# A GNN layer on one Trainium2 core: raw groups 112 chunks apart, in-degrees counted from 656 bytes at a looked-up place, fewer chunks by columns and rows

## The chip, the cores and the metric

The kernel runs on one core of one Trainium2 chip. TensorE (PE) multiplies matrices, VectorE (DVE) and ScalarE (ACT) work element by element, GpSimd (POOL) issues the indirect DMAs that gather rows by index, and SyncE (SP) issues plain DMAs. Each engine takes its instructions in program order and waits for others through semaphores. The metric is the device time of one execution, in microseconds (us); lower is better.

## The reference

`x` holds 12500 rows of 128 values, `src` and `dst` 200000 edges sorted by `dst`. With H = 512:

```python
h = max(layernorm(x), 0)
agg = segment_sum(h[src], dst, 12500)
deg = segment_sum(ones, dst, 12500)
agg = agg / max(deg, 1)
a = relu(agg @ Wg + h @ Ws + bg)
a = tanh(a @ W1 + b1)
a = tanh(a @ W2 + b2)
out = x + a @ W3 + b3
```

## The kernel before

**Set-up.** `windowed` normalises `x` into a table `htab` in DRAM (lines 205 to 290) and turns the edge indices into columns of 128. The edges are cut into 1563 chunks of 128. As `dst` is sorted and has 16 edges for a node on the average, chunk c falls into a narrow window of nodes around 8c (`window`, 144 nodes wide at first). `htab` is ready some 95 us after the start.

**One chunk.** Its 128 source rows are brought to SBUF, VectorE builds a one-hot matrix of the destinations in the window (`onehot`, L438, eight chunks at a time, three buffers), and TensorE multiplies rows by one-hot and adds the product to the block's sums in PSUM (`add`; all matmuls show as L342 and all transposes as L345, the lines of a helper). A block is 512 nodes; the last ones are smaller.

**Four ways to bring rows.**

- Gathered: POOL issues one indirect DMA for the chunk (`gather`, L352, tile `rows`), at most `AHEAD` = 19 chunks ahead. The pool `rows_in` has that many buffers, and a buffer is free when the chunk's `add` is done.
- Raw: ten groups of eight chunks, `STEP` apart from chunk 256 on, are gathered from `x` itself (L167) before `htab` is there, and normalised on VectorE during chunks 16 to 95 (`centre`, L209 to L216).
- By rows: SP issues 128 plain DMAs of one row each (`row_loads`, tile `srows`; all plain DMAs after the set-up show as L348). It reads the addresses 32 at a time into registers (`offsets`, L363, TENSOR_LOAD). Four buffers.
- By columns: ScalarE or VectorE copies 128 columns out of `tab`, a transposed table in SBUF, with addresses from registers (`column_copies`, L398), and TensorE transposes the result (`turn`).

`LANES` says which of every eighth chunk goes to which of the last two ways: S rows, A ScalarE, V VectorE, - gathered. `load_times` spreads the loads of a lane over the chunks before their use: it takes the places of the lane's chunks in the order of the gathered ones, extends them to the front by `SBUFS - 1` steps for the row lane, and clamps each due time to at least 1. In chunk c all that is due by the count `behind` of gathered chunks done is issued.

**The table `tab`.** `own(s)` (SP) loads 512 rows of `htab` into a tile `xb`, two buffers; `own_turned(s)` transposes it on TensorE, ScalarE copies it to `tab`. Before, this is done for one block in every fourth chunk, from chunk 2 on.

**In-degrees.** The low byte of each `dst` lies in DRAM (`bytes_at`). For each tile of 128 nodes `seen` (SP) loads, for every node, the 2416 bytes in which its edges must lie, and `tallied` (VectorE, L452) counts the bytes equal to the node's; this comes at every 14th chunk, two tiles ahead. `count` turns degrees into a row for a block. `checked` and `outside` see whether any edge lies outside of its window (then `general`, another routine, runs; it doesn't here).

**MLP and the order of work.** A block's four layers are a generator, `layers`, with planned costs. Up to chunk `QUICK` = 1312 one step of it is emitted in every second chunk (`go_on`). From there on a planner compares `now`, the planned time of TensorE, with `there`, the time at which a chunk's rows are planned to arrive (7.5 + 1.251 for each gather), and emits MLP steps until the rows are there. TensorE's, ScalarE's and SP's instructions in this part keep the order of emission.

Of the kernel before, what the change touches and what calls it, by code (L numbers as in the profile page):

```python
# [22 lines left out]
F32 = mybir.dt.float32  # L23
BF16 = mybir.dt.bfloat16
I32 = mybir.dt.int32
U8 = mybir.dt.uint8
AF = mybir.ActivationFunctionType
ALU = mybir.AluOpType
# [8 lines left out]
GRP = 8  # L37
NRAW = 10
RAW0 = 256
STEP = 40  # L40
AHEAD = 19
LATE = 12
LEAD = 16
QUICK = 1312
EVERY = 8
AT = 3
LANES = "AVASA-AVAVA-SAV"
FROM, UNTIL = 152, 1540
SBUFS = 4
MARGIN = 18  # L50
TOGETHER = 4
# [10 lines left out]

TILE_EVERY = 14
PAST = 255


NCOPY = 4
# [4 lines left out]
def windowed(ctx, tc, x, src, dst, Wg, Ws, bg, W1, b1, W2, b2, W3, b3, out, flag):  # L72
# [26 lines left out]
    def first(w, span=per):  # L99
        return (span - w) // 2  # L100
# [5 lines left out]
        return per * c + first(w), w  # L106

    each = E // N
    low_w, wide_w = first(WINDOWS[0][1]), WINDOWS[0][1]
    back = each * (low_w + wide_w - 1)  # L110
    reads = -(-(back - each * low_w + P) // each) * each
    assert each * N == E and each * per == P and reads <= each * (PAST + 1)
    assert all(first(w) >= low_w and first(w) + w <= low_w + wide_w for _, w in WINDOWS)
    pad_dst = 2 * N // (PAST + 1) * (PAST + 1) + PAST
    assert pad_dst >= 2 * N - PAST and NT * P - N <= P
    ended = (E - (reads - back)) // each
    assert not any(n % (PAST + 1) == PAST and (each * n < back or n > ended) for n in range(N))

    lanes = ([], [], [])
    for i, c in enumerate(c for c in range(AT, NCH, EVERY) if FROM <= c < UNTIL and not raw(c)):  # L120
# [64 lines left out]
    def flat(t):  # L185
        return t.rearrange("p a b -> p (a b)")

    htab = dram.tile([NP, D], F32, name="htab")
    bytes_at = dram.tile([back + NROW * ROW + reads], U8, name="bytes_at")
    tab = const.tile([P, NP], F32, name="tab")  # L190
    scol = const.tile([P, NCOL], I32, name="scol")
    ROWB = 4 * D
# [3 lines left out]
    oh_bufs = [const.tile([P, GRP, WINDOWS[0][1]], F32, name=f"oh{i}") for i in range(OHS)]  # L196
    near = const.tile([P, NRAW, GRP], F32, name="near")
    degs = const.tile([P, NT], F32, name="degs")
    parity = const.tile([P, 2], F32, name="parity")
    for i in range(2):  # L200
        nc.vector.tensor_scalar(parity[:, i : i + 1], jp[:, :1], -1.0, float(i * P), op0=ALU.mult, op1=ALU.add)
# [23 lines left out]
    with tc.tile_pool(name="setup", bufs=1) as sp, tc.tile_pool(name="ln", bufs=2) as ln:  # L225

        def indices(name, a, pad, keep):
            r = sp.tile([NROW, ROW], I32, name="idx_raw")

            nc.vector.memset(r, pad)  # L230
            even = FULL // 16 * 16
            for s0, s1 in ((0, even), (even, FULL)):
                if s1 > s0:
                    nc.scalar.dma_start(r[s0:s1, :], a[s0 * ROW : s1 * ROW].rearrange("(p e) -> p e", e=ROW))
            nc.scalar.dma_start(r[FULL : FULL + 1, :REST], a[FULL * ROW : E].rearrange("(p e) -> p e", p=1))
            if name == "src":
                some = r.rearrange("r (q p) -> r q p", p=P)[:, AT::EVERY]
                for to, step, first_at in zip(places, (ROWB, 4), (0, TAB_AT)):
                    nc.vector.tensor_scalar(to, some, float(step), float(first_at), op0=ALU.mult, op1=ALU.add)
            else:  # L240
                r8 = flat(oh_bufs[0]).bitcast(U8)[:NROW, :ROW]
                nc.scalar.copy(r8, r.bitcast(U8).rearrange("r (e b) -> r e b", b=4)[:, :, 0])
                end = back + NROW * ROW
                nc.scalar.dma_start(bytes_at[back:end].rearrange("(r e) -> r e", e=ROW), r8)
                past = flat(oh_bufs[1]).bitcast(U8)[:1, : max(back, reads)]
                nc.vector.memset(past, PAST)
                nc.scalar.dma_start(bytes_at[:back].rearrange("(o e) -> o e", o=1), past[:, :back])
                nc.scalar.dma_start(bytes_at[end:].rearrange("(o e) -> o e", o=1), past[:, :reads])
            rf = sp.tile([NROW, ROW], F32, name="idx_f")
            nc.vector.tensor_copy(rf, r)  # L250
            for q0 in range(0, CPR, 4):
                p = ps_m.tile([P, 4, P], F32, name="pm")
                for q in range(4):
                    nc.tensor.transpose(p[:, q, :NROW], rf[:, (q0 + q) * P : (q0 + q + 1) * P], ident[:NROW, :NROW])  # L254
                keep(q0, p[:, :, :NROW].rearrange("p q r -> p r q"))
# [91 lines left out]
    def sp_dma(*a):  # L347
        tc.keep_in_program_order(nc.sync.dma_start(*a))  # L348
# [84 lines left out]
    def onehot(g):  # L433
# [7 lines left out]
        )]  # L441
        ohs[g] = oh

    def seen(t):

        w = ed.tile([P, reads], U8, name="nearby", bufs=2)
        sp_dma(w, bass.AP(tensor=bytes_at.tensor, offset=bytes_at.offset + t * P * each, ap=[[each, P], [1, reads]]))
        nearby[t] = w

    def tallied(t):  # L450
        w = nearby.pop(t)
        done = nc.vector.tensor_scalar(  # L452
            w, w, parity[:, t % 2 : t % 2 + 1], None, op0=ALU.is_equal, op1=ALU.add, accum_out=degs[:, t : t + 1]
        )
        if newest:
            tc.add_manual_dep(
                done.ins, newest[0].ins.name,
                mybir.DependencyInfo(mybir.DependencyClass.NoSync, mybir.DependencyReason.DATA), reason="issue_after",
            )
        if t % 4 == 3 or t == NT - 1:  # L460
            d = degs[:, t // 4 * 4 : t + 1]
            nc.vector.tensor_scalar(d, d, 1.0, None, op0=ALU.max)
            nc.vector.reciprocal(d, d)

    def checked():

        u = dloc[:, RAW0:RAW1].rearrange("p (u k) -> p u k", k=STEP)
        wide = WINDOWS[0][1]
        ends = [c for c, _ in WINDOWS[1:]] + [NCH - 1]
        parts = [(dloc[:, :RAW0], wide), (u[:, :, GRP:], wide), (u[:, :, :GRP], W_RAW), (near, wide)]  # L470
        parts += [(dloc[:, RAW1 : ends[0]], wide)]
        parts += [(dloc[:, c0:c1], w) for (c0, w), c1 in zip(WINDOWS[1:], ends[1:])]
        parts += [(dloc[:LAST, NCH - 1 : NCH], WINDOWS[-1][1])]
        k = len(parts)
        ext = const.tile([P, 2, k], F32, name="ext")
        nc.vector.memset(ext, 0.0)
        for i, (part, w) in enumerate(parts):
            rows = LAST if i == k - 1 else P
            axis = AX.XY if len(part.shape) == 3 else AX.X
            nc.vector.tensor_reduce(ext[:rows, 0, i : i + 1], part, axis, ALU.min)  # L480
            nc.vector.tensor_reduce(ext[:rows, 1, i : i + 1], part, axis, ALU.max)
            e = ext[:rows, 1, i : i + 1]
            nc.vector.tensor_scalar(e, e, -1.0, float(w - 1), op0=ALU.mult, op1=ALU.add)
        worst = const.tile([P, 1], F32, name="worst")
        nc.vector.tensor_reduce(worst, ext, AX.XY, ALU.min)
        nc.vector.tensor_scalar(worst, worst, 0.0, None, op0=ALU.is_lt)
        return worst

    def outside(worst):
        p = flat(ps_m.tile([P, 4, P], F32, name="pm"))  # L490
        pe.matmul(p[:1, :1], worst, ident_ones, start=True, stop=True)
        nc.vector.tensor_copy(flag, p[:1, :1])

    reach = [[] for _ in blocks]
    for c in range(NCH):
# [243 lines left out]
    def soonest():  # L739
        two = work[: 2 if len(work) > 1 and work[1][3] < work[0][3] and work[0][4] else 1]  # L740
        return min(two, key=lambda w: max(w[2], now), default=None)
# [12 lines left out]
    own(1)  # L754
    own_turned(0)
    own(2)
    seen(0)
    seen(1)
    onehot(0)
    onehot(1)  # L760
    counted = 0
    for c in range(NCH):
        g = c // GRP
# [2 lines left out]
        if c % GRP == 0 and g + 2 < ngrp:  # L766
            onehot(g + 2)
            if raw((g + 2) * GRP):
                raw_scaled(((g + 2) * GRP - RAW0) // STEP)
            copies, times = loading[2]  # L770
            while times and times[0] <= behind:
                times.pop(0)
                next(copies, 0)
            if g == 2 + NRAW + 2:
                worst = checked()
            if g == 2 + NRAW + 4:
                outside(worst)
            if 2 <= g < 2 + NRAW:
                centre(ed, raw_rows[g - 2], GRP, raw_stats(g - 2), bufs=1)
            if g == 2 + NRAW:  # L780
                factors(stats_raw)
# [15 lines left out]
        if c >= QUICK:  # L797

            there = 7.5 + 1.251 * (NRAW * GRP + order.index(c)) if c not in apart else 0
            while soonest() and max(now, soonest()[2]) < there:  # L800
                go_on(soonest())
            now = max(now, there) + 0.27
# [10 lines left out]

        if c % TILE_EVERY == 1 and c // TILE_EVERY < NT:
            tallied(c // TILE_EVERY)
            if c // TILE_EVERY + 2 < NT:
                seen(c // TILE_EVERY + 2)
        if c % 4 == 2 and c // 4 + 1 < nown:
            own_turned(c // 4 + 1)
            if c // 4 + 3 < nown:  # L820
                own(c // 4 + 3)
        if c < QUICK:
            if c % 2 == 0:
                go_on(work[0] if work else None)
# [380 lines left out]
```

## Time and profile before

| what | before |
|---|---|
| median of 3 runs | 1818.41 us (1816.91 to 1819.31) |
| the profiled execution | 1817.22 us |
| its span, first to last instruction | 1815.4 us |
| mean granted TensorE clock | 0.889 |
| HBM traffic | 147.49 MB read, 13.03 MB written |
| DMA packets | 135577, 163.06 MB |

All times in the profile are those of one execution on the chip. A group's row gives the line in the kernel, the engine, the operation, the tile written and read, the count, the busy time in us and the mean of one in ns, and then how long the engine was idle before these instructions and what ended that. A row of the timeline gives the start and the duration in us; PE rows count two instructions for one matmul in fp32. A row of busy time by stretches gives PE, PEld (weight loads), DVE, ACT and POOL, each with the count of instructions, and then the granted clock, the share of the DMA engines and GB/s. The page's chain of work that ended last gives DMA 26%, PE 24%, issue 20%, ACT 16% and POOL 8%.

### The profile page before, as it was taken

The page shows a single profiled execution, that of the slowest core. Times are in us where ns is not written, and L with a number is a line of the kernel's source. Part 1 is how long each engine was busy: PE and PEld are TensorE (multiplying, and loading weights), DVE is VectorE, ACT ScalarE, POOL GpSimd, SP SyncE. Part 2 cuts the span into 40 slices and gives each one's busy share as a digit, 9 for nine tenths or more (in the row PEclk, how much of TensorE's full clock was granted, in tenths as well). Part 3 has the DMA queues.
Part 4 walks back from the last instruction along what each step waited for, and adds up shares of the span by engine and source line. Part 5 has one row for each costly group of instructions (what it writes and reads, how often), then busy time and mean ns, then how long its engine had stood idle before and what let it go on. Part 6 is the DMA issues. An engine that isn't in the chain of part 4 may idle for free.

```text
span 1815.4 us, 36659 instructions
## 1 busy us (share of the span) xinstructions
PE 1299.8 (72%) x5031; PEld 812.2 (45%) x5031; DVE 1152.6 (63%) x6351; ACT 1187.4 (65%) x10333; POOL 1348.7 (74%) x1429
## 2 busy tenths in 40 slices
PE   0046767777888787877777777777777767698598
PEld 0035544444555554444444444444444344454457
DVE  7946845668677788766756666756666764644411
ACT  1201145867878788878777777778768865777763
POOL 7777777777777777777777777777777776777773
PEclk9996565989898899989999889989889998798899
DMA  8844423233333332332332332332333323222221
GB/s 211 235 140 112 122 68 80 75 81 81 81 94 94 86 102 75 94 88 74 84 84 75 87 88 75 86 82 76 86 81 81 92 71 86 67 72 66 65 59 37
DMA packets 135577, 163.06 MB, mean 90 GB/s; under 512 B 32934, under 2 KB 99107, under 8 KB 135128
## 3 DMA queue, kind: packets, MB, share of 16 engines
q0 software_dynamic: 45472, 93.22, 20.4%
q1 hardware_dynamic: 86574, 63.90, 12.4%
q10 hardware_dynamic: 3276, 3.51, 0.7%
q14 instruction: 213, 1.74, 0.3%
q8 instruction: 42, 0.69, 0.2%
HBM read 147.49 MB, written 13.03 MB: 88 GB/s over the span
## 4 chain that ended last, share of the span: by engine, by line
DMA 26%; PE 24%; issue 20%; ACT 16%; POOL 8%; DVE 3%; ACTq 1%; DVEq 0%; POOLq 0%
DMA rows<-htab,scol 26%; ACT cols L398 14%; PE pm L342 14%; PE agg L342 7%; POOL rows L352 4%; POOL raw L167 4%; PE edge L342 2%; ACT h L416 2%; DVE cols L398 1%; DVE nearby L452 1%; DVE oh L438 1%; ACTq L363 1%; PE pt L345 1%; PE pm L345 0%; DVEq L363 0%
## 5 line engine op out<-in xcount | busy, mean ns | idle before, releaser
L352 POOL DMA_INDIRECT rows<-htab,scol x1341 | 1270.7, 948 | 416.7 <-issue 230.2
L398 ACT COPY cols<-tab 128x4 uint8 x9856 | 996.4, 190 | 283.3 <-issue 231.7
L342 PE MATMUL pm<-h,w 128*128 128x512 f32 (+4 forms) x1344 | 648.3, 580 | 36.1 <-ACT h L416 22.2
L342 PE MATMUL agg<-oh,rows 128*128 128x144 f32 (+3 forms) x1914 | 474.9, 352 | 231.7 <-DMA rows<-htab,scol 224.3
L342 PEld LDWEIGHTS agg<-oh,rows 128*128 128x128 f32 x1914 | 353.6, 224 | 509.1 <-DMA rows<-htab,scol 370.2
L398 DVE COPY cols<-tab 128x4 uint8 x5504 | 432.2, 196 | 164.1 <-issue 142.9
L438 DVE TENSOR_TENSOR oh<-shared,dloc 128x1152 f32<-128x1152 f32 (+2 forms) x186 | 245.7, 1322 | 358.0 <-PE agg L342 217.1
L452 DVE TENSOR_SCALAR_CACHE_REDUCE nearby<-nearby,parity 128x2416 uint8<-128x2416 uint8 x98 | 266.2, 2717 | 4.8 <-DMA nearby<-bytes_at 4.8
L342 PEld LDWEIGHTS pm<-h,w 128*128 128x128 f32 x1344 | 222.1, 204 | 60.2 <-ACT h L416 26.5
L342 PE MATMUL edge<-oh,rows 128*128 128x144 f32 (+2 forms) x768 | 178.6, 332 | 80.9 <-DMA rows<-htab,scol 80.1
L342 PEld LDWEIGHTS edge<-oh,rows 128*128 128x128 f32 x768 | 131.7, 209 | 192.7 <-DMA rows<-htab,scol 126.7
L416 ACT ACTIVATE h<-pm,b2c 128x512 f32<-128x512 f32 (+4 forms) x112 | 70.2, 626 | 63.9 <-PE pm L342 63.8
L419 ACT COPY tab<-pt 128x512 f32<-128x512 f32 (+1 forms) x25 | 14.4, 577 | 127.2 <-PE pt L345 127.2
L167 POOL DMA_INDIRECT raw<-in_x_dram,rsrc x80 | 77.1, 964 | 25.6 <-issue 23.5
L416 ACT ACTIVATE h<-pm,b1c 128x512 f32<-128x512 f32 (+4 forms) x112 | 68.9, 627 | 29.1 <-PE pm L342 28.7
L254 PE MATMUL pm<-ident,idx_f 98*128 98x98 f32 x32 | 6.2, 376 | 77.8 <-DVE agg L220 47.5
L345 PE MATMUL pm<-ident,cols 128*128 128x128 f32 x120 | 35.6, 297 | 32.1 <-DVE rd L511 15.7
L342 PEld LDWEIGHTS agg<-oh,turned 128*128 128x128 f32 x176 | 36.6, 227 | 36.5 <-issue 24.7
L342 PE MATMUL agg<-oh,turned 128*128 128x144 f32 (+1 forms) x176 | 42.4, 328 | 11.3 <-ACT turned L419 11.3
L573 DVE TENSOR_TENSOR mT<-agg,sums 128x136 f32<-128x136 f32 (+6 forms) x57 | 15.2, 271 | 40.6 <-PE agg L342 31.3
L254 PEld LDWEIGHTS pm<-ident,idx_f 98*128 98x128 f32 x32 | 5.1, 223 | 78.6 <-issue 47.8
L688 DVE TENSOR_TENSOR o<-pt,xb 128x512 f32<-128x512 f32 x23 | 15.7, 681 | 35.3 <-PE pt L345 34.9
(90 smaller groups left out, 632.6 us busy)
## 6 DMA issues: line engine op xcount, KB each, us to landing
srows<-htab SPq DMA_DIRECT2D x2816, 0.5 KB
nearby<-bytes_at SPq DMA_DIRECT2D x98, 302.0 KB
rows<-htab,scol POOLq DMA_INDIRECT x1341
xb<-htab SPq DMA_DIRECT2D x24, 256.0 KB
xb<-in_x_dram SPq DMA_DIRECT2D x23, 256.0 KB
out_dram<-o SPq DMA_DIRECT2D x23, 256.0 KB
xt<-in_x_dram SPq DMA_DIRECT2D x7, 704.0 KB
htab<-h SPq DMA_DIRECT2D x7, 704.0 KB
```

Of the source, the lines that this page charges most:

```text
L167: nc.gpsimd.indirect_dma_start(out=t[:, j, :], out_offset=None, in_=x, in_offset=bass.IndirectOffsetOnAxis(ap=rsrc[:, g, j : j + 1], axis=0),)
L342: tc.keep_in_program_order(nc.tensor.matmul(*a, **k))
L345: tc.keep_in_program_order(nc.tensor.transpose(*a, **k))
L352: nc.gpsimd.indirect_dma_start(out=r, out_offset=None, in_=htab, in_offset=bass.IndirectOffsetOnAxis(ap=scol[:, c : c + 1], axis=0),)
L363: loads, vs = nc.values_load_multi_w_load_instructions(places[min(lane, 1)][r : r + 1, q // EVERY, p0 : p0 + LOADS], engines=[kind], min_v ...
L398: done = tc.keep_in_program_order(copy(tb[:, 4 * p : 4 * p + 4], tbytes[:, bass.ds(v - TAB_AT, 4)]))
L416: tc.keep_in_program_order(nc.scalar.activation(*a, **k))
L419: tc.keep_in_program_order(nc.scalar.copy(*a))
L438: newest[:] = [nc.vector.tensor_tensor(oh[:, :k, :w], lane[:, None, :w].to_broadcast([P, k, w]), dloc[:, g * GRP : g * GRP + k][:, :, None ...
L452: done = nc.vector.tensor_scalar(w, w, parity[:, t % 2 : t % 2 + 1], None, op0=ALU.is_equal, op1=ALU.add, accum_out=degs[:, t : t + 1])
L573: nc.vector.tensor_tensor(out, s, t, op=ALU.add)
L688: nc.vector.tensor_tensor(o[:, :whole], po[:, :whole], xb[:, :whole], op=ALU.add)
```

## The change

- Raw groups are 112 chunks apart in place of 40, so they reach to chunk 1376; `AHEAD` is 21.
- `LANES` becomes `A--A-SA---` from chunk 104 on: 17 chunks by rows, 51 by ScalarE's columns and none by VectorE's. Before it was 22, 77 and 43.
- In-degrees: `told_begins` counts, from the first `dst` of each chunk, how many chunks begin before a tile of nodes, and so finds where the tile's bytes begin. `seen` reads that place into a register of SP and loads 656 bytes for a node there. `seen` is three tiles ahead and has four buffers. `outside` also checks that the degrees add up to the number of edges, and moves from chunk 128 to the last tile's tally.
- `own` and `own_turned` come in every second chunk, from chunk 1 on.
- At chunk `QUICK` the planner's clock is set to `there - SPREAD`.

```diff
-STEP = 40
-AHEAD = 19
+STEP = 112
+AHEAD = 21
 LATE = 12
 LEAD = 16
 QUICK = 1312
+SPREAD = 8
...
-LANES = "AVASA-AVAVA-SAV"
-FROM, UNTIL = 152, 1540
+LANES = "A--A-SA---"
+FROM, UNTIL = 104, 1540
...
+MAY_BE_OFF = 240
+SEEN = 656
+TOLD = 14
+EARLY = 3
...
+            if name == "dst":
+                nc.vector.tensor_copy(firsts, rf.rearrange("r (q p) -> r q p", p=P)[:, :, 0])
...
+    def told_begins():
+
+        less = flat(ed.tile([P, GRP, W_RAW], F32, name="ohr", bufs=1)).bitcast(U8)
+        less = less[:NROW, : NT * CPR].rearrange("r (t q) -> r t q", q=CPR)
+        nc.vector.scalar_tensor_tensor(
+            less, firsts[:, None, :].to_broadcast([NROW, NT, CPR]), 1.0 / P,
+            lane[:NROW, :NT, None].to_broadcast([NROW, NT, CPR]), op0=ALU.mult, op1=ALU.is_lt,
+        )
+        many = degs[:NROW, :]
+        nc.vector.tensor_reduce(many, less, AX.X, ALU.add)
+        p = flat(ps_m.tile([P, 4, P], F32, name="pm"))
+        pe.matmul(p[:1, :NT], ident_ones[:NROW], many, start=True, stop=True)
+        nc.vector.tensor_scalar(begins, p[:1, :NT], float(P), float(ahead_of - P - MAY_BE_OFF), op0=ALU.mult, op1=ALU.add)
+
+    told = {}
+
     def seen(t):
 
-        w = ed.tile([P, reads], U8, name="nearby", bufs=2)
-        sp_dma(w, bass.AP(tensor=bytes_at.tensor, offset=bytes_at.offset + t * P * each, ap=[[each, P], [1, reads]]))
+        if t % TOLD == 0:
+            u = min(t + TOLD, NT)
+            loads, vs = nc.values_load_multi_w_load_instructions(
+                begins[:1, t:u], engines=[mybir.EngineType.SP], min_val=0, max_val=NCH * P,
+                skip_runtime_bounds_check_because="a count of chunks is at most the number of chunks",
+            )
+            for ld in loads:
+                tc.keep_in_program_order(ld)
+            told.update(enumerate(vs, t))
+        w = ed.tile([P, SEEN], U8, name="nearby", bufs=4)
+        at_v = bytes_at[bass.ds(told.pop(t), (P - 1) * each + SEEN)]
+        sp_dma(w, bass.AP(tensor=at_v.tensor, offset=at_v.offset, ap=[[each, P], [1, SEEN]]))
         nearby[t] = w
...
-    seen(0)
-    seen(1)
     onehot(0)
     onehot(1)
+    told_begins()
+    for t in range(EARLY):
+        seen(t)
...
+            if c == QUICK:
+                now = there - SPREAD
...
             tallied(c // TILE_EVERY)
-            if c // TILE_EVERY + 2 < NT:
-                seen(c // TILE_EVERY + 2)
-        if c % 4 == 2 and c // 4 + 1 < nown:
-            own_turned(c // 4 + 1)
-            if c // 4 + 3 < nown:
-                own(c // 4 + 3)
+            if c // TILE_EVERY == NT - 1:
+                outside(worst)
+            if c // TILE_EVERY + EARLY < NT:
+                seen(c // TILE_EVERY + EARLY)
+        if c % 2 == 1 and c // 2 + 1 < nown:
+            own_turned(c // 2 + 1)
+            if c // 2 + 3 < nown:
+                own(c // 2 + 3)
```

More of the change, by code (lines that the diff above doesn't have):

```diff
@@ L108, in windowed @@
     each = E // N
[L109 to L113, printed above, removed]
+    spans = [(first(W_RAW, per * GRP) - per * GRP, W_RAW + per * GRP), *((first(w) - per, w + per) for _, w in WINDOWS)]
+    off = max(max(-f, f + w) for f, w in spans)
+    ahead_of = P + MAY_BE_OFF
+    past_end = P * (each + 1) + SEEN
     pad_dst = 2 * N // (PAST + 1) * (PAST + 1) + PAST
-    assert pad_dst >= 2 * N - PAST and NT * P - N <= P
-    ended = (E - (reads - back)) // each
-    assert not any(n % (PAST + 1) == PAST and (each * n < back or n > ended) for n in range(N))
+    assert each * N == E and pad_dst >= 2 * N - PAST and 0 < NT * P - N < P
+    under, over = off + -(-ahead_of // each), off + -(-(SEEN - MAY_BE_OFF) // each)
+    assert off + max(under, over) <= PAST
+    assert all(under <= n <= N - over or n % (PAST + 1) != PAST for n in range(N))
     lanes = ([], [], [])
@@ L188, in windowed @@
     htab = dram.tile([NP, D], F32, name="htab")
-    bytes_at = dram.tile([back + NROW * ROW + reads], U8, name="bytes_at")
+    bytes_at = dram.tile([ahead_of + NROW * ROW + past_end], U8, name="bytes_at")
     tab = const.tile([P, NP], F32, name="tab")
@@ L198, in windowed @@
     degs = const.tile([P, NT], F32, name="degs")
+    found = const.tile([P, NT], F32, name="found")
+    firsts = const.tile([NROW, CPR], F32, name="firsts")
+    begins = const.tile([1, NT], I32, name="begins")
     parity = const.tile([P, 2], F32, name="parity")
@@ L242, in indices @@
                 nc.scalar.copy(r8, r.bitcast(U8).rearrange("r (e b) -> r e b", b=4)[:, :, 0])
-                end = back + NROW * ROW
-                nc.scalar.dma_start(bytes_at[back:end].rearrange("(r e) -> r e", e=ROW), r8)
-                past = flat(oh_bufs[1]).bitcast(U8)[:1, : max(back, reads)]
+                end = ahead_of + NROW * ROW
+                nc.scalar.dma_start(bytes_at[ahead_of:end].rearrange("(r e) -> r e", e=ROW), r8)
+                past = flat(oh_bufs[1]).bitcast(U8)[:1, : max(ahead_of, past_end)]
                 nc.vector.memset(past, PAST)
-                nc.scalar.dma_start(bytes_at[:back].rearrange("(o e) -> o e", o=1), past[:, :back])
-                nc.scalar.dma_start(bytes_at[end:].rearrange("(o e) -> o e", o=1), past[:, :reads])
+                nc.scalar.dma_start(bytes_at[:ahead_of].rearrange("(o e) -> o e", o=1), past[:, :ahead_of])
+                nc.scalar.dma_start(bytes_at[end:].rearrange("(o e) -> o e", o=1), past[:, :past_end])
             rf = sp.tile([NROW, ROW], F32, name="idx_f")
             nc.vector.tensor_copy(rf, r)
+            if name == "dst":
+                nc.vector.tensor_copy(firsts, rf.rearrange("r (q p) -> r q p", p=P)[:, :, 0])
             for q0 in range(0, CPR, 4):
@@ L452, in tallied @@
         done = nc.vector.tensor_scalar(
-            w, w, parity[:, t % 2 : t % 2 + 1], None, op0=ALU.is_equal, op1=ALU.add, accum_out=degs[:, t : t + 1]
+            w, w, parity[:, t % 2 : t % 2 + 1], None, op0=ALU.is_equal, op1=ALU.add, accum_out=found[:, t : t + 1]
         )
@@ L460, in tallied @@
         if t % 4 == 3 or t == NT - 1:
-            d = degs[:, t // 4 * 4 : t + 1]
-            nc.vector.tensor_scalar(d, d, 1.0, None, op0=ALU.max)
-            nc.vector.reciprocal(d, d)
+            some = slice(t // 4 * 4, t + 1)
+            nc.vector.tensor_scalar(degs[:, some], found[:, some], 1.0, None, op0=ALU.max)
+            nc.vector.reciprocal(degs[:, some], degs[:, some])
     def checked():
@@ L483, in checked @@
             nc.vector.tensor_scalar(e, e, -1.0, float(w - 1), op0=ALU.mult, op1=ALU.add)
-        worst = const.tile([P, 1], F32, name="worst")
-        nc.vector.tensor_reduce(worst, ext, AX.XY, ALU.min)
-        nc.vector.tensor_scalar(worst, worst, 0.0, None, op0=ALU.is_lt)
+        worst = const.tile([P, 2], F32, name="worst")
+        nc.vector.tensor_reduce(worst[:, :1], ext, AX.XY, ALU.min)
+        nc.vector.tensor_scalar(worst[:, :1], worst[:, :1], 0.0, None, op0=ALU.is_lt)
         return worst
     def outside(worst):
+        k = N - (NT - 1) * P
+        nc.vector.tensor_reduce(worst[:, 1:], found[:, : NT - 1], AX.X, ALU.add)
+        nc.vector.tensor_tensor(worst[:k, 1:], worst[:k, 1:], found[:k, NT - 1 :], op=ALU.add)
         p = flat(ps_m.tile([P, 4, P], F32, name="pm"))
-        pe.matmul(p[:1, :1], worst, ident_ones, start=True, stop=True)
-        nc.vector.tensor_copy(flag, p[:1, :1])
+        pe.matmul(p[:1, :2], ident_ones, worst, start=True, stop=True)
+        missed = const.tile([1, 1], F32, name="missed")
+        nc.vector.tensor_scalar(missed, p[:1, 1:2], float(E), None, op0=ALU.not_equal)
+        nc.vector.tensor_tensor(flag, p[:1, :1], missed, op=ALU.max)
     reach = [[] for _ in blocks]
@@ L775, in windowed @@
                 worst = checked()
-            if g == 2 + NRAW + 4:
-                outside(worst)
             if 2 <= g < 2 + NRAW:
```

## The prediction

> **What bounds the kernel now.** I read the page's table of engines first, then busy time by stretches, then GpSimd's groups and its timeline.
>
> ```profile
> PE 1299.8 (72%) x5031; PEld 812.2 (45%) x5031; DVE 1152.6 (63%) x6351; ACT 1187.4 (65%) x10333; POOL 1348.7 (74%) x1429
> ```
>
> ```profile
> 40.00:100.00 60.00, 4.19 (x20) 3.25 (x20) 54.32 (x74) 13.63 (x16) 45.45 (x48) 1.00 0.86 231
> 600.00:700.00 100.00, 78.88 (x325) 49.27 (x326) 81.16 (x467) 80.40 (x717) 75.61 (x80) 0.95 0.35 93
> 1740.00:1780.00 40.00, 38.08 (x200) 28.58 (x199) 8.33 (x29) 19.42 (x117) 29.40 (x32) 1.00 0.24 63
> ```
>
> ```profile
> L352 POOL DMA_INDIRECT rows<-htab,scol x1341 | 1270.7, 948 | 416.7 <-issue 230.2 <-PE agg L342 86.8 <-DMA rows<-htab,scol 36.0
> L167 POOL DMA_INDIRECT raw<-in_x_dram,rsrc x80 | 77.1, 964 | 25.6 <-issue 23.5 <-DMA rsrc<-in_src_dram 1.8 <-DMA xb<-htab 0.3
> ```
>
> ```profile
> 3.06 1.09 POOL L167 DMA_INDIRECT raw<-in_x_dram,rsrc  x1 [1.51 <-DMA rsrc<-in_src_dram]
> ...
> 1523.16 0.94 POOL L352 DMA_INDIRECT rows<-htab,scol  x1 [0.30 <-issue]
> 1524.40 0.95 POOL L352 DMA_INDIRECT rows<-htab,scol  x1 [0.30 <-PE pm L342]
> 1532.15 0.94 POOL L352 DMA_INDIRECT rows<-htab,scol  x1 [6.80 <-PE agg L342]
> ...
> 1747.01 0.94 POOL L352 DMA_INDIRECT rows<-htab,scol  x1 [1.46 <-PE edge L342]
> ...
> 1790.68 0.94 POOL L352 DMA_INDIRECT rows<-htab,scol  x1 [0.30 <-issue]
> ```
>
> The first table shows no engine above 74%, which hides the bound. POOL's column in the stretches shows it: 48 gathers in 60 us, 80 in 100 us and 32 in 40 us are 1.25 us each, whether VectorE is busy for 91%, 81% or 21% of the stretch and whether the DMA engines are at 0.86 or 0.24. A gather takes 0.94 us and the next begins 0.30 us after it, and that gap belongs to the gather: it stands there even when nothing is late. From 3.06 to 1790.68 POOL issues 80 + 1341 = 1421 gathers, so 1420 intervals fill 1787.6 us. At 1.249 us each they need 1773.6; 14.0 us are stalls, of which 6.5 is the gap before 1532.15, 1.2 that before 1747.01 and the rest gathers that ran long. So the time is gathers x 1.249 + stalls + head and tail, and everything else matters only where it stops POOL or stretches the tail of 24.7 us from 1790.68 to the span's end.
>
> **Gathers added: +92.4 us.** Of 1563 chunks 80 are raw and the rest are gathered unless a lane takes them. Before, the lanes took 22 by rows, 77 by ScalarE and 43 by VectorE, 142 in all, which leaves the 1341 of the row above. Afterwards they take 17 + 51 + 0 = 68, which leaves 1415. That is 74 more x 1.249 = 92.4 us. No cover exists: POOL has no idle time but the stalls. The other side of this trade, and the tally, are these groups:
>
> ```profile
> L398 ACT COPY cols<-tab 128x4 uint8 x9856 | 996.4, 190 | 283.3 <-issue 231.7
> L398 DVE COPY cols<-tab 128x4 uint8 x5504 | 432.2, 196 | 164.1 <-issue 142.9
> L452 DVE TENSOR_SCALAR_CACHE_REDUCE nearby<-nearby,parity 128x2416 uint8<-128x2416 uint8 x98 | 266.2, 2717 | 4.8 <-DMA nearby<-bytes_at 4.8
> ```
>
> VectorE loses its 432 us of copies and, with 656 bytes for 2416, about 98 x 2717 x (1760/2416) ns = 194 us; ScalarE loses 26 of 77 chunks, about 336 us. Neither is on POOL's path, so the credit is zero except through the stalls and the tail below. The bounds are 0 and those two items.
>
> **A jam on SP at the start: +34 us.** This is the dearest edit after the gathers. `load_times` gives the row lane four buffers and starts loading three steps ahead. The first row chunk is now 147, 145 ordered chunks into the run, and the step is (1361 - 145) // 16 = 76 chunks, so the first load would be due at 145 - 228 = -83. All due times up to 1 are clamped to 1. That makes 36 bunches of four due at chunk 0, and one more falls due at chunk 1: 148 row DMAs ahead of the table tile that `own(3)` loads in chunk 1. Before, the first was due at chunk 14 and nothing bunched. The built order of SP's queue has it so: three `xb`, the new read of `begins`, three `nearby`, 148 `srows` with five address reads, `nearby`, and only then the fourth `xb`. TensorE, in program order, transposes that tile right after the add of chunk 5, since `own_turned` now comes every second chunk. The prices:
>
> ```profile
> 94.20 5.07 SPq L348 DMA_DIRECT2D xb<-htab  x3
> 97.78 1.08 PE L345 MATMUL pt<-ident,xb 128*128 128x128 f32 x4 [13.77 <-DVE ext L481]
> 99.32 6.96 SPq L348 DMA_DIRECT2D nearby<-bytes_at  x3
> 104.58 0.94 POOL L352 DMA_INDIRECT rows<-htab,scol  x1 [0.30 <-issue]
> ...
> 107.26 0.71 PE L342 MATMUL agg<-oh,rows 128*128 128x76 f32 x2 [8.39 <-DMA rows<-htab,scol]
> ...
> 120.70 1.06 PE L345 MATMUL pt<-ident,xb 128*128 128x128 f32 x4
> 121.55 1.46 PE L342 MATMUL agg<-oh,rows 128*128 128x144 f32 x4
> 128.72 3.55 SPq L348 DMA_DIRECT2D srows<-htab  x8
> ```
>
> ```profile
> 138.50 0.94 POOL L352 DMA_INDIRECT rows<-htab,scol  x1 [0.30 <-DMA rows<-htab,scol]
> ```
>
> ```profile
> 1509.16 8.38 SPq L348 DMA_DIRECT2D srows<-htab  x24
> ```
>
> ```profile
> L363 SPq TENSOR_LOAD <-place x88: 2032/2178/2658, 122.2 to 1612.0; - x88
> ```
>
> A row DMA costs 8.38 / 24 = 0.35 us when bunched, early in the run 3.55 / 8 = 0.44. An address read costs 2.18. The jam is 148 x 0.35 + 5 x 2.2 = 63 us (76 at the early price). `begins` needs three VectorE steps and a matmul behind the tile transposed at 97.78, so SP reads it near 99.8, about when it issued `nearby` before, and with 2.2 for the read and three issues the jam starts near 103. It ends near 166; the fourth tile is issued near 166.5 and lands 3.6 us later, as the first did (94.20 to 97.78). Transposes (1.06) and two matmuls (half of 1.46) free the buffer of chunk 6 near 172. POOL has 21 buffers and six are freed by chunks 0 to 5, so it stops before gather number 27, counted from the 0th at 104.58; that one ran at 138.50. The stall is 172 - 138.5 = 34 us, with 28 and 47 as its ends.
>
> **Aftermath: +3 us.** TensorE then stands a full buffer set behind while 21 more tiles come at every second chunk. Two adds and a tile are 1.46 + 1.06 = 2.5 us, POOL's 2.50 for two, so it neither gains nor loses; address reads in SP's queue make some tiles late. I take 3, between 0 and 10. The tiles end at chunk 49 and TensorE catches up before the MLP is due.
>
> **Other edits.**
>
> ```profile
> L209 DVE TENSOR_REDUCE agg<-xt 128x11 f32<-128x1408 f32 x7 | 11.4, 1625 | 3.5 <-DMA xt<-in_x_dram 3.4
> ```
>
> `told_begins` adds an is_lt and a sum over 98 x 1568 and a one-column matmul. By this row the two take 2 x 1.625 x 1568/1408 = 3.6 us. They run while TensorE waits for its first row (8.39 us before 107.26) and cost 0 there; without that cover, 4 us. Seven reads of `begins`, 2.2 us each on SP, hide in its idle time. `outside` moves to chunk 1359, where TensorE waits for the last tally with the adds of later chunks queued behind it; 21 x 1.249 = 26 us of buffers cover a wait of a few us, so 0 (bound 5). Raw groups 112 apart change no count.
>
> **QUICK and tail: -7.7 and -6.5 us.**
>
> ```profile
> 1511.29 16.46 PE L342 MATMUL pm<-h,w 128*128 128x512 f32 x32 [3.97 <-ACT turned L419]
> ```
>
> ```profile
> 1708.38 0.85 PE L342 MATMUL agg<-oh,turned 128*128 128x144 f32 x2 [6.87 <-ACT turned L419]
> ```
>
> ```profile
> 1801.66 0.30 PE L342 MATMUL agg<-oh,rows 128*128 128x20 f32 x2
> ```
>
> At chunk 1312 the planner's clock `now` lies far behind `there`, and every MLP step that waits is emitted at once: this is the 16.46 us and what held POOL for 6.5. With `now = there - 8` at most 8 us are bunched and two more buffers stand behind them, so that stall goes. The later 1.2 goes as well: it is the trail of a wait for ScalarE's columns (6.87 us at 1708.38), which have 8 chunks left after 1312 where they had 14. The last add runs 11.0 us after its gather (1801.66 against 1790.68); the first does 2.7 after. A TensorE that isn't behind should do it in 4.5, so I take 6.5 off the tail, between 0 and 8.3.
>
> **The sum.** 1817.2 (the profiled execution: span 1815.4 and 1.8 around it) + 92.4 + 34 + 3 - 7.7 - 6.5 = 1932.4. The median of the runs is 1.2 above the profiled execution, less than any term here, so 1932 it is.
>
> **A rule weighed.**
>
> ```profile
> 151.52 1.22 DVE L215 TENSOR_TENSOR ohr<-raw 128x1024 f32<-128x1024 f32 x1
> 151.57 1.99 POOL L352 DMA_INDIRECT rows<-htab,scol  x1 [0.30 <-issue]
> ```
>
> Here a gather ran 1.05 us long beside a VectorE product of two SBUF tiles; ten such products stay in the program. The Trainium skill, "SBUF — State Buffer", section "Who interferes with whom", says that such an instruction, and copies in a two-port mode, shut GpSimd out of a port pair until they end. By that rule the 5504 copies that go could have held gathers back, and POOL's pace would improve. The row of L352 bounds it: its mean is 948 ns against 0.94 us undisturbed, so all lengthening together is 1341 x 8 ns = 11 us, and the trace does not bear the rule out for these copies.
>
> **Rivals.**
> - The jam is hidden, because SP drains it faster than its rows say or the tile isn't needed so soon: 1932 - 37 = 1895. The fixed order of three queues speaks against it. 8%.
> - The jam lasts: each pair of tiles waits for landing, four rows and an address read, 3.6 + 0.5 + 4 x 0.35 + 2.2 = 7.7 us in place of 5.0, for 10 pairs: 1932 + 27 = 1959. Against it: an address read comes only every eighth bunch. 9%.
> - Faster than before: the 0.30 us between gathers is queueing that the removed copies and row DMAs cause. From a pace of 1.249 - 115/1495 = 1.172 the kernel would break even; with 0.15 of the gap gone it would take 1932 - 224 = 1708. The stretches with VectorE at 21% and 91% at one pace speak against it. 3%.
> - VectorE's share of the pace is real but small (the rule above): 1932 - 11 = 1921, inside the forecast's own range.
>
> **How the numbers follow.** The forecast has 80% with that last case, and about 1915 to 1950 of its own: the jam from 28 to 47, the aftermath from 0 to 10, the tail from -8.3 to 0. I take 1908 to 1950 as the range, which leaves out nearly all of the hidden jam, the lasting one and the faster case. About 0.2% is what a measurement here tells from no change; every case but the faster one is far above it: faster 3%, same 1%, slower 96%.
>
> **What would show it.** GpSimd's group `rows` should count 1415 at a mean near 948; one idle gap of about 34 us should stand before a gather near 138 us, with the fourth `xb` late on SP behind 148 `srows`; no gap near chunk 1312; the last add some 4 to 5 us after the last gather. A pace other than 1.249, or a fourth tile landing before 130 us, would make it wrong.

## The result and the profile after

The changed kernel takes 1924.99 us (median of 4 runs, 1924.24 to 1926.4) against 1818.38 us before: a ratio of 1.0588, with a 95% interval of 1.057 to 1.0606. It is slower by 106.6 us; 1932 was forecast, and 1908 to 1950 as the range. The profiled execution took 1926.4 us, with a span of 1924.6.

The page of the changed kernel: the engines, and from its costliest groups those that answer to the ones shown of before.

```profile
PE 1337.6 (70%) x4964; PEld 796.4 (41%) x4964; DVE 564.5 (29%) x854; ACT 866.5 (45%) x6936; POOL 1419.1 (74%) x1503
...
L362 POOL DMA_INDIRECT rows<-htab,scol x1415 | 1341.1, 948 | 462.2 <-issue 256.7
L408 ACT COPY cols<-tab 128x4 uint8 x6528 | 663.2, 190 | 215.5 <-issue 191.4
...
L488 DVE TENSOR_SCALAR_CACHE_REDUCE nearby<-nearby,parity 128x656 uint8<-128x656 uint8 x98 | 86.9, 886 | 0.3 <-DMA nearby<-bytes_at 0.3
```

VectorE works 588 us less and ScalarE 321 us less than before, and the kernel is slower. POOL's gathers grew from 1341 to 1415 at the same mean of 948 ns. Its timeline shows the rest (start and duration in us; in brackets the idle time before a gather and what ended it).

```profile
3.03 1.09 POOL L172 DMA_INDIRECT raw<-in_x_dram,rsrc  x1 [1.49 <-DMA rsrc<-in_src_dram]
...
135.73 0.94 POOL L362 DMA_INDIRECT rows<-htab,scol  x1 [0.30 <-issue]
136.97 0.94 POOL L362 DMA_INDIRECT rows<-htab,scol  x1 [0.30 <-issue]
168.74 0.94 POOL L362 DMA_INDIRECT rows<-htab,scol  x1 [30.82 <-PE agg L352]
...
181.58 0.94 POOL L362 DMA_INDIRECT rows<-htab,scol  x1 [0.66 <-PE agg L352]
...
1906.57 0.94 POOL L362 DMA_INDIRECT rows<-htab,scol  x1 [0.30 <-PE pm L352]
```

From 3.03 to 1906.57 there are 1494 intervals in 1903.5 us. At 1.249 they need 1866.0, so 37.5 us are stalls: 30.5 is the one gap before 168.74, 0.4 that before 181.58, and the rest gathers that ran long, as before. The tail from 1906.57 to the span's end is 18.0 us, where it was 24.7. So the difference of the spans, 109.2 us, is 92.4 for 74 gathers, + 23.5 of stalls, - 6.7 of the tail.

The gap's cause stands in SP's and PE's timelines of the changed kernel.

```profile
95.46 4.85 SPq L358 DMA_DIRECT2D xb<-htab  x3
102.16 1.32 SPq L358 DMA_DIRECT2D nearby<-bytes_at  x3
105.56 57.84 SPq L358 DMA_DIRECT2D srows<-htab  x148
163.50 0.37 SPq L358 DMA_DIRECT2D nearby<-bytes_at  x1
163.97 0.41 SPq L358 DMA_DIRECT2D xb<-htab  x1
```

```profile
113.36 0.78 PE L352 MATMUL agg<-oh,rows 128*128 128x116 f32 x2 [0.51 <-DMA rows<-htab,scol]
166.96 1.09 PE L355 MATMUL pt<-ident,xb 128*128 128x128 f32 x4 [52.82 <-DMA xb<-htab]
167.84 1.07 PE L352 MATMUL agg<-oh,rows 128*128 128x124 f32 x4
...
1910.21 0.30 PE L352 MATMUL agg<-oh,rows 128*128 128x20 f32 x2
```

The sixth add ends at 114.1. TensorE then stands 52.8 us for the fourth table tile, which SP issues at 163.97, behind 148 row DMAs. POOL has 21 buffers, runs to gather number 26 (136.97) and stops. The gap that it shows is shorter than TensorE's by the buffers that were still free. The last row shows the tail: the last add starts 3.6 us after its gather, where it was 11.0.

### The profile page after: what moved, and what is told of

Its sections match the earlier page's. It is cut to its first block, busy times and chain, and to the rows that moved or that the text cites. A ratio compares the mean times of both kernels' runs of the same rounds, so it can differ in the third digit from the quotient of the medians.

```text
span 1924.6 us, 26263 instructions
## 1 busy us (share of the span) xinstructions
PE 1337.6 (70%) x4964; PEld 796.4 (41%) x4964; DVE 564.5 (29%) x854; ACT 866.5 (45%) x6936; POOL 1419.1 (74%) x1503
## 4 chain that ended last, share of the span: by engine, by line
DMA 34%; issue 28%; PE 25%; POOL 5%; DVE 3%; SPq 3%; ACT 0%; POOLq 0%; DVEq 0%; ACTq 0%
DMA rows<-htab,scol 31%; PE pm L352 14%; PE agg L352 8%; POOL rows L362 5%; PE edge L352 2%; SPq L358 2%; DMA xt<-in_x_dram 2%; DMA xb<-htab 2%; PE pt L355 1%; PE pm L355 1%; SPq L373 1%; DVE h L231 1%; DVE agg L217 0%; DVE agg L224 0%; DVE oh L448 0%
## 5 line engine op out<-in xcount | busy, mean ns | idle before, releaser
L362 POOL DMA_INDIRECT rows<-htab,scol x1415 | 1341.1, 948 | 462.2 <-issue 256.7
L408 ACT COPY cols<-tab 128x4 uint8 x6528 | 663.2, 190 | 215.5 <-issue 191.4
L352 PE MATMUL agg<-oh,rows 128*128 128x144 f32 (+3 forms) x2030 | 523.5, 356 | 287.2 <-DMA rows<-htab,scol 282.0
L352 PEld LDWEIGHTS agg<-oh,rows 128*128 128x128 f32 x2030 | 369.1, 220 | 628.6 <-DMA rows<-htab,scol 492.5
L352 PE MATMUL edge<-oh,rows 128*128 128x144 f32 (+2 forms) x800 | 202.0, 343 | 118.8 <-DMA rows<-htab,scol 117.6
L488 DVE TENSOR_SCALAR_CACHE_REDUCE nearby<-nearby,parity 128x656 uint8<-128x656 uint8 x98 | 86.9, 886 | 0.3 <-DMA nearby<-bytes_at 0.3
L355 PE MATMUL pt<-ident,xb 128*128 128x128 f32 x98 | 21.0, 352 | 83.5 <-DMA xb<-htab 69.6
L426 ACT ACTIVATE h<-pm,b3c 128x512 f32<-128x512 f32 (+4 forms) x28 | 17.7, 633 | 100.3 <-PE pm L352 100.3
L426 ACT ACTIVATE h<-pm,bgc 128x512 f32<-128x512 f32 (+4 forms) x28 | 17.7, 633 | 79.5 <-PE pm L352 79.5
L553 DVE COPY rd<-pm 128x512 f32<-128x512 f32 (+4 forms) x28 | 17.4, 623 | 86.7 <-PE pm L355 86.7
```

Source lines behind the costliest of these rows:

```text
L352: tc.keep_in_program_order(nc.tensor.matmul(*a, **k))
L355: tc.keep_in_program_order(nc.tensor.transpose(*a, **k))
L362: nc.gpsimd.indirect_dma_start(out=r, out_offset=None, in_=htab, in_offset=bass.IndirectOffsetOnAxis(ap=scol[:, c : c + 1], axis=0),)
L408: done = tc.keep_in_program_order(copy(tb[:, 4 * p : 4 * p + 4], tbytes[:, bass.ds(v - TAB_AT, 4)]))
L426: tc.keep_in_program_order(nc.scalar.activation(*a, **k))
L488: done = nc.vector.tensor_scalar(w, w, parity[:, t % 2 : t % 2 + 1], None, op0=ALU.is_equal, op1=ALU.add, accum_out=found[:, t : t + 1])
```

## Experiments

Eight kernels were made. Two sets of four (e1, e2, e3 and e8, and the same kernels again as f1 to f4) ran where every kernel took longer: the one before over a third (2466.47 and 2488.57 us), the changed one without the jam a fifth (e1 and f1, beside e4, e6 and e7). Their times are compared within their set alone, and the last section says what was different. The other set (e4 to e7) ran beside a kernel before of 1816.21 us.

**The jam undone (e1, f1; also a part of e4, e6 and e7).** Loads of the row lane begin two steps ahead in place of three:

```diff
-        use = [max(FROM - 46 + MARGIN, use[0] - step), *use] if lane else [use[0] - step * k for k in range(SBUFS - 1, 0, -1)] + use
+        use = [max(FROM - 46 + MARGIN, use[0] - step), *use] if lane else [use[0] - step * k for k in range(2, 0, -1)] + use
```

> The row lane's loads begin two steps ahead of their use in place of three, so 20 row DMAs stand ahead of the fourth table tile on SP and not 148. Theory (that tile held TensorE, and TensorE's buffers held POOL): the idle gap of 30.8 us before gather 27 goes and nothing takes its place, 1925 - 31 = 1894 us. Rival (the gap is only where a loss shows that the early tiles, now twice as dense, cause anyway): over 1910 us, with new gaps between 110 and 200 us.

> The kernel of e1 again, beside a kernel before that takes some 1818 us: the row lane's loads begin two steps ahead, 20 row DMAs stand ahead of the fourth table tile. Theory: the gap of 30.8 us before gather 27 goes, nothing takes its place, 1894 to 1896 us (e4, e6 and e7, which also have it, took 1895.5). Rival (new gaps between 110 and 200 us): over 1910 us.

**Fewer buffers (e2, f2).** The jam stays, POOL has 15 buffers:

```diff
-AHEAD = 21
+AHEAD = 15
```

> The changed kernel with 15 row buffers for 21; SP's queue is the same. Theory: POOL stops six gathers earlier and goes on at the same moment near 169 us, so the gap grows by 6 x 1.249 = 7.5 us to 38.3 and the time to 1932.5 us. Rival (POOL waits for SP's queue or for DMAs in flight, not for buffers): the gap keeps its place and 1925 us stays.

> The kernel of e2 again: the changed kernel with 15 row buffers for 21. Theory (buffers hold POOL, and SP's queue sets when it goes on): the gap begins six gathers earlier and ends at the same moment near 169 us, 38.3 us for 30.8, and 1932.5 us. Rival (POOL waits for SP's queue itself): the gap keeps its place, 1925 us.

Measured: e1 2261.17 us and e2 2301.59 us (ratios to before 0.9165, 0.9123 to 0.9207, and 0.933, 0.9296 to 0.9364); again, f1 2279.77 and f2 2321.08 us (0.917 and 0.9321). The expected times could not be met there, but the places of the gaps could. SP and POOL of e1:

```profile
126.72 30.39 SPq L358 DMA_DIRECT2D srows<-htab  x20
157.21 0.37 SPq L358 DMA_DIRECT2D nearby<-bytes_at  x1
157.68 0.41 SPq L358 DMA_DIRECT2D xb<-htab  x1
```

```profile
162.41 0.95 POOL L362 DMA_INDIRECT rows<-htab,scol  x1 [11.23 <-PE agg L352]
```

And of e2:

```profile
128.54 74.09 SPq L358 DMA_DIRECT2D srows<-htab  x148
202.73 0.37 SPq L358 DMA_DIRECT2D nearby<-bytes_at  x1
203.19 0.41 SPq L358 DMA_DIRECT2D xb<-htab  x1
```

```profile
207.85 0.94 POOL L362 DMA_INDIRECT rows<-htab,scol  x1 [62.75 <-PE agg L352]
```

In e1 the gap stands before gather number 27 = 6 + 21, in e2 before number 21 = 6 + 15 (f1 and f2 the same): the buffers set where it begins. It ends 4.7 us after the fourth `xb` is issued in both (157.68 to 162.41, 203.19 to 207.85), and 4.8 in the changed kernel (163.97 to 168.74), over moments of issue that lie 46 us apart: SP's queue sets where it ends. That is the theory's chain, and the rival that POOL waits for SP's queue itself falls, since the gap did not keep its place. But in e1 a gap of 11.23 us is left, as its 20 row DMAs took 30.39 us there; that the gap can go altogether, only the other set shows.

What the jam is worth was seen in the other set, whose kernels e4, e6 and e7 contain its cure. SP of e4:

```profile
104.58 6.98 SPq L358 DMA_DIRECT2D srows<-htab  x20
111.66 0.37 SPq L358 DMA_DIRECT2D nearby<-bytes_at  x1
112.12 0.41 SPq L358 DMA_DIRECT2D xb<-htab  x1
```

The fourth tile is issued at 112.12, and no gap of POOL follows: between two gathers of e4, e6 or e7 POOL is never idle for more than 0.32 us. The three spans are 1893.9, 1892.7 and 1893.1 us against 1924.6: 30.7 to 31.9 us for a gap of 30.5. The medians lie 29.4 to 29.7 us under the changed kernel's, which ran beside a kernel before that was 2.2 us slower. So within some 3 us no other loss hides behind the gap.

**The new clock left out (e4).** The cure above, and:

```diff
-            if c == QUICK:
-                now = there - SPREAD
```

> The changed kernel without the jam on SP (loads two steps ahead) and without the new clock at chunk 1312. Theory (the MLP burst held POOL for 6.5 us with 19 buffers): the burst of about 20 us comes back, two more buffers cover 2.5 us of it, 1894 + 4 = 1898 us. Rival (with fewer columns on ScalarE the burst is covered whole): 1894 us.

Measured: 1895.59 us (ratio 1.0438, 1.0421 to 1.0456), as e6 and e7, which keep the clock. PE and POOL of e4:

```profile
1582.18 13.90 PE L352 MATMUL pm<-h,w 128*128 128x512 f32 x32
...
1596.35 3.60 PE L352 MATMUL pm<-h,w 128*128 128x512 f32 x8
```

```profile
1597.05 0.94 POOL L362 DMA_INDIRECT rows<-htab,scol  x1 [0.30 <-issue]
1598.30 0.94 POOL L362 DMA_INDIRECT rows<-htab,scol  x1 [0.30 <-PE pm L352]
```

The burst is back, 17.8 us of it, but POOL goes on in its pace. The tail is short too, as the last gather and the last add show:

```profile
1875.48 0.94 POOL L362 DMA_INDIRECT rows<-htab,scol  x1 [0.30 <-PE pm L352]
```

```profile
1879.36 0.30 PE L352 MATMUL agg<-oh,rows 128*128 128x20 f32 x2
```

The last add starts 3.9 us after its gather, and 18.4 us remain to the span's end (1893.9). The rival holds: with 21 buffers and fewer columns the burst is covered, and the new clock is worth nothing in this kernel. Which of the change's other edits covers it was not tried.

**The new clock alone (e5).** The kernel before with this and `SPREAD = 8`:

```diff
+            if c == QUICK:
+                now = there - SPREAD
```

> The kernel before with the planner's clock set to 8 us ahead of the rows at chunk 1312, and nothing else. Theory (the burst costs 6.5 us; the gap of 1.2 us near 1747 us and the long tail come from ScalarE's columns): 1818.4 - 6.5 = 1812 us, with the last add still 8 to 11 us after its gather. Rival (the burst made the tail long too): 1804 us.

Measured: 1802.53 us, 0.9925 of before (0.9909 to 0.9942), so 13.7 us less. POOL near the old stall and at the end, and the last add, of e5:

```profile
1531.71 0.95 POOL L353 DMA_INDIRECT rows<-htab,scol  x1 [0.30 <-issue]
1532.96 0.94 POOL L353 DMA_INDIRECT rows<-htab,scol  x1 [0.30 <-PE agg L343]
...
1782.81 0.94 POOL L353 DMA_INDIRECT rows<-htab,scol  x1 [0.30 <-PE pm L343]
```

```profile
1787.37 0.30 PE L343 MATMUL agg<-oh,rows 128*128 128x20 f32 x2
```

The gap of 6.8 us near 1532 is gone, and so is the long tail: the last add starts 4.6 us after its gather, and 18.1 us remain to the span's end (1800.9). The gap of 1.46 near 1747 is gone too: between two gathers POOL is never idle for more than 0.32 us. So is TensorE's wait of 6.87 us for ScalarE's columns, which ended at 1708.38 in the kernel before. The same add, ahead of the same product of `tab` and `ws`, in e5:

```profile
1694.87 0.69 PE L343 MATMUL agg<-oh,turned 128*128 128x144 f32 x2
1695.35 1.92 PE L343 MATMUL pm<-tab,ws 128*128 128x512 f32 x2
```

All this fell with the clock alone, while all 77 chunks by ScalarE's columns stayed. Here the rival was right: 1804 was its figure. This version is also the fastest measured beside a kernel before of 1816 us.

**The tally doubled and more (e6).** The cure, and two counts more of each tile into results that nothing uses:

```diff
+        w2 = ed.tile([P, SEEN], U8, name="nearby2", bufs=1)
+        for i in range(2):
+            nc.vector.tensor_scalar(
+                w2, w, parity[:, t % 2 : t % 2 + 1], None, op0=ALU.is_equal, op1=ALU.add, accum_out=again[:, i : i + 1]
+            )
```

> The changed kernel without the jam on SP, and with two more counts of each tile's bytes on VectorE, whose results are not used: 2 x 98 x 0.886 = 174 us more of VectorE. Theory (the in-degree work is off the path at either size): 1894 us, within 2. Rival (VectorE's counts delay one-hots and so TensorE): over 1900 us.

Measured: 1895.45 us (ratio 1.0439, 1.0422 to 1.0457). VectorE and POOL of e6:

```profile
L491 DVE TENSOR_SCALAR_CACHE_REDUCE nearby<-nearby,parity 128x656 uint8<-128x656 uint8 x196 | 175.2, 894 | 151.4 <-DMA nearby<-bytes_at 148.0
```

```profile
L363 POOL DMA_INDIRECT rows<-htab,scol x1415 | 1339.1, 946 | 431.4 <-issue 263.1 <-PE agg L353 68.9 <-DMA rows<-htab,scol 49.1
```

175 us more of VectorE cost nothing. In this kernel the in-degree work is off the path, and so the change's saving there brought nothing.

**Raw groups 40 apart (e7).** The cure and `STEP = 40`.

> The changed kernel without the jam on SP and with the raw groups 40 chunks apart as before; the lanes take 68 chunks again. Theory (where the raw groups stand changes no count of gathers): 1894 us, within 3. Rival (closer groups let TensorE fall behind or run ahead so that POOL stops): over 1900 us or under 1888.

Measured: 1895.32 us (ratio 1.0437, 1.042 to 1.0455): the place of the raw groups changes nothing.

**The old lanes, and denser ones (e3, f3 and e8, f4).** The change with other lanes (the second pattern is that of e8):

```diff
-LANES = "A--A-SA---"
-FROM, UNTIL = 104, 1540
+LANES = "AVASA-AVAVA-SAV"
+FROM, UNTIL = 152, 1540
...
+LANES = "AVASAVAVAVAVSAV"
```

> The changed kernel with the lanes of before (22 chunks by rows, 77 by ScalarE, 43 by VectorE, from chunk 152 on); everything else stays changed. Theory (1.249 us for each gather, whatever the other engines do): 1341 gathers again, 1925 - 92.4 - 31 = 1802 us, with the mean of a gather near 948 ns. Rival (VectorE's copies stretch gathers): up to 11 us more, 1813. Second rival (late columns bring back the wait near chunk 1312 and the long tail): 1816.

> The kernel of e3 again: the change with the lanes of before. Theory (1.249 us for each gather; the stall at chunk 1312 and the long tail are gone as in e5): 1341 gathers, 1925 - 92.4 - 31 = 1802 us, no different from e5, mean of a gather 945 to 950 ns. Rival (VectorE's copies stretch gathers beside the other changes): up to 1813.

> As the kernel with the lanes of before, but VectorE also takes the 22 chunks of that pattern that were left to POOL (65 for 43): 1319 gathers. Theory: 96 gathers fewer than the changed kernel, 1925 - 119.9 - 31 = 1774 us. Rival (the column copies come too late and TensorE waits for them): gaps of POOL after 400 us and 1780 to 1800 us.

> The kernel of e8 again: as f3, but VectorE also takes the 22 chunks left to POOL, 1319 gathers. Theory: 22 x 1.249 = 27.5 us under f3, 1774 us. Rival (VectorE's or ScalarE's columns come too late, TensorE waits and fills the buffers): gaps of POOL after 400 us, 1780 to 1800 us.

Measured: e3 2424.32 us (0.9828 of before, 0.9794 to 0.9863), e8 2407.99 us (0.9754, 0.9705 to 0.9802); again, f3 2457.53 (0.9873) and f4 2442.9 us (0.9796). Both miss their expected times by over 600 us, under the conditions that the last section describes, so neither 1802 nor 1774 us was tested, and the denser lanes stay open. The price of a gather is measured in the other set all the same: e5 with 1341 gathers and e4, e6, e7 with 1415 lie 92.8 to 93.1 us apart, and 74 x 1.249 = 92.4. These kernels differ in other edits as well, but in none of the four is POOL idle for more than 0.32 us between two gathers: from the first gather to the last it takes 1779.62 us in e5 and 1872.43 in e4, 92.8 more, so the count sets the difference.

## Why the prediction was right, point by point

- **The bound.** POOL's pace of 1.249 us for each gather holds in both kernels, and 588 us less of VectorE did not shorten it: the mean is 948 ns before and after. So the rivals by which the removed copies had stretched gathers fall. The rule for copies in a two-port mode that the prediction weighs from the Trainium skill ("SBUF — State Buffer", "Who interferes with whom") shows no effect here: 5504 copies went and the mean stayed. Whether they ran in such a mode no view here shows. What does lengthen gathers is the square of a raw group, as in the pair of rows that the prediction quotes, and it still does after the change (first pair); a one-hot, whose input `shared` lies in PSUM, does not (second pair):

```profile
191.44 1.22 DVE L223 TENSOR_TENSOR ohr<-raw 128x1024 f32<-128x1024 f32 x1
191.56 1.93 POOL L362 DMA_INDIRECT rows<-htab,scol  x1 [0.30 <-PE agg L352]
...
604.56 1.36 DVE L448 TENSOR_TENSOR oh<-shared,dloc 128x1152 f32<-128x1152 f32 x1 [3.06 <-PE agg L352]
605.23 0.94 POOL L362 DMA_INDIRECT rows<-htab,scol  x1 [0.30 <-issue]
```

After the change nine gathers begin during such a square, and all take longer (1.04 to 1.93 us); 163 begin during a one-hot of this size, and none takes more than 0.95 us.

- **74 gathers, +92.4.** Shown, by the count and by e5 against e4, e6 and e7.
- **The jam, +34.** Right in mechanism, in its place to the gather, and 3.5 us too large: 30.5. The queue took 60 us from the end of the three `nearby` to the next one (103.48 to 163.50; forecast 63), and the tile landed 3.0 us after its issue (163.97 to 166.96). The 3.6 came from the first of three tiles issued together.
- **The aftermath, +3.** Mis-sized: one gap of 0.66, so 0.4, and the rival of a lasting jam falls with it. TensorE's two adds and a tile went faster than 2.5 us once the rows were there (1.09 and 1.07 us in the rows above, which overlap; the next tile begins at 168.85, 1.89 us after the first).
- **QUICK and tail, -7.7 and -6.5.** The sums are right: both gaps are gone and the tail is 6.7 us shorter. The split among the edits was not as forecast. The prediction gave the gap of 6.8 to the clock and the two buffers, and put the gap of 1.46 near 1747 and the wait of 6.87 us before it down to ScalarE's columns. But e5 removed both gaps and the long tail with the clock alone, while every column stayed, and e4 has none of them without the clock, with the burst back. So either the clock or the change's other edits are enough, and the loss needed both the burst at chunk 1312 and the old kernel around it. The sum holds whichever edit does it, and so it doesn't prove the split. By which steps TensorE carried the delay for 250 chunks was not followed.
- **Edits priced at nothing** (the tally, the raw groups, `told_begins`, `outside`) were free: e6 and e7 tried the first two, and the profile after has no new gap of POOL but those before 168.74 and 181.58.
- **The sum** was 1932.4 against 1926.4 for the profiled execution; the 6 us are the jam (3.5) and the aftermath (2.6).

## What to carry to other kernels

When one engine issues at a fixed pace without idle time, count its instructions first: here 74 more of them cost 92 us, and 900 us of work taken from other engines brought nothing back. When a start time is computed and then clamped, look for what piles up at the clamp, and follow it along in-order queues to the buffers: the stall is the time of the pile less the buffers that were free. A gain that goes with two changes made at once should be tried with each of them alone before it is put down to one: here either alone brought all of it.

## What the runs showed of the hardware

In the two slower sets the instructions themselves came late. ScalarE's timeline in e1, which contains the same copies as e4:

```profile
709.70 0.19 ACT L408 COPY cols<-tab 128x4 uint8 x1 [1.21 <-issue]
710.40 0.19 ACT L408 COPY cols<-tab 128x4 uint8 x1 [0.51 <-issue]
711.10 0.19 ACT L408 COPY cols<-tab 128x4 uint8 x1 [0.51 <-issue]
711.82 0.19 ACT L408 COPY cols<-tab 128x4 uint8 x1 [0.53 <-issue]
...
714.66 2.10 ACT L408 COPY cols<-tab 128x4 uint8 x21 [1.04 <-issue]
```

The waits of ScalarE for nothing that the profile shows, in e1 and in e4 (us in total, how many, the longest):

```profile
ACT cols L408 <- issue: 778.8, 1166, 1.9
```

```profile
ACT cols L408 <- issue: 193.9, 181, 1.9
```

In e4 the same copies follow each other without a gap (the profile writes such a run as one row):

```profile
714.79 1.99 ACT L408 COPY cols<-tab 128x4 uint8 x20
```

A copy takes 0.19 us in both, but in this stretch of e1 each begins some 0.70 us after the one before, where e4 does 20 of them in 1.99 us. The delays come and go: from 714.66 on e1 too does 21 copies in 2.10 us. SP's first 20 row DMAs took 30.39 us in e1 and 6.98 in e4. The mean granted clock was 0.789 in e1 and 0.89 in e4. Under these conditions the trade of copies for gathers turned round: e1, with 68 chunks by lanes, took 2261 us and e3, with 142, took 2424, while fewer gathers should have made e3 the faster. So the trade that costs 92 us in the one condition is a gain in the other. The number of copies alone does not order the kernels: e8, with 22 more chunks by VectorE than e3, took 2408. What e3 and e8 share are 77 chunks by ScalarE, and the chain of work that ended last gives ScalarE 47% in e3 and 42% in e8, 22% in e1, and 0% in e4. That late copies on ScalarE made the lanes dear there fits this, but no run changed ScalarE's share alone. Why instructions came late was not found.
